# Zero point terms written ahead of a pair's products, and four token tiles transposed by DMA

## The chip, the cores and the metric

The kernel runs on one core of one Trainium2 chip. The metric is the device time of one execution in microseconds (us). The core has a matmul engine (PE, also TensorE, with its weight loads listed as PEld), a vector engine (DVE, VectorE), a scalar engine (ACT, ScalarE), a general engine (POOL, GpSimd), and SP (SyncE), whose queue here only issues DMAs. Each engine works through its own instructions strictly in order and waits on semaphores for the others. A DMA is issued from the queue of SP or of ACT and moves its data beside the engines.

## The reference

For each of two batches, x has 1024 tokens of 2048 elements, and ctx is 2048 by 2048. The first step is a quantised product, the second a linear layer with low-rank additions:

```
q1 = fake_quant(layernorm(x), x1_scale, x1_zp)     # clip(round(v / s + z), 0, 255), then (q - z) * s
q2 = fake_quant(ctx, x2_scale, x2_zp)
x  = x + q1 @ q2                                    # K = 2048, N = 2048
z  = layernorm(x)
x  = x + z @ kernel + bias + B_eff (A_eff z) + B_sh (A_sh z)
```

The kernel has both quantised operands as whole numbers from 0 to 255 less 128, which bf16 holds exactly, so the product of the codes is exact. The zero points come in as a sum: with d1 = 128 - z1 and d2 = 128 - z2, the product of the true values is s1 * s2 times (the product of the codes, plus d1 times the sum of each column of q2's codes, plus d2 times the sum of each row of q1's codes, plus 2048 * d1 * d2). This addition is called the zero point term here.

## The kernel before

**Tiling.** The 1024 tokens of a batch are 8 token tiles of 128 (m = 0 to 7), in four groups g of two tiles (MG = 2). The 2048 columns are four blocks n of 512. x and the running result live in four buffers y[g]. All of a batch's ctx codes for one column block are in two big buffers c2[n]; two column blocks are held at a time.

**Preparing x** is `prep_x(b, m)`. DVE takes the statistics of the layer norm (L283) and works out a scale and an offset. ACT quantises the tile to eight bits (L295, into q8, of which there are two that take turns), then recentres each half of 1024 elements to bf16 (L298, into qh, of which there is one) and sums it on the way. PE transposes each half in eight blocks of 128 by 128 into a psum tile pt (L303), and DVE copies that to c1T[g] (L304), the left operand of the product. The two sums give r_s, the row part of the zero point term (L306 to L308).

**Preparing ctx** is `quantise` (ACT L314, then DVE L317), eight calls for one column block, each on a 512 KB load that SP's queue issues ahead into ten buffers `lit`; `load_next` issues the next load when one is used up. `column_term` sums the columns on PE (pcp, L333), copies them with DVE (L343), adds the four partial sums on PE (pc, L345) and writes the column part of the zero point term to colt[n] with DVE (L348).

**The product** is `xattn_pair(b, n, g)`: one psum tile pa of two halves, one for each token tile j of the group. ACT writes the zero point term colt[n] + r_s[m] into a half (L359, at high priority), and 16 bf16 matmuls of 128x128 by 128x512 add to what stands there (L361, start=False). DVE adds the scaled pair to y (L370) and takes statistics of the result. Three psum tiles (acc1, delta, acc0) take turns for the pairs.

**The layer after it** is `ffn`: f32 matmuls of 128x128 by 128x512 (L611) in a seven by seven scheme of products of sums of blocks; o counts the outer products and s the inner ones. DVE spreads each result into y (L629), and finished blocks are sent to `out` by DMAs from ACT's queue (L631). While the layer of batch 0 ends (o = 6), `meanwhile` prepares batch 1: tiles m = 0 to 3 of x at s = 1 to 4, the ctx codes of its first column block at s = 0 to 3, its column term at s = 3, and the codes of the next block at s = 4 to 6. After it come the pairs of batch 1, with tiles 4 to 7 prepared between the pairs of column blocks 0 and 1, as in batch 0.

**What sets the order.** The Python code is written in one sequence, but a scheduler at build time decides the order in each engine's queue, by readiness and priority, with dependencies tracked by tile. The order is then fixed in the program; on the chip every queue keeps it.

Of the kernel before, what the change touches and what calls it, by code (L numbers as in the profile page):

```python
# [66 lines left out]
def tile_quant_xattn_then_lora_ffn(  # L67
# [17 lines left out]
    nc = tc.nc  # L85
    B, S, D = x.shape
    KT = D // P
    MT = S // P
# [8 lines left out]
    MG = GT // P  # L97
    H = D // 2
    KH = KT // 2
# [36 lines left out]
    def bf(t, n):  # L136

        return t.rearrange("p k n -> p (k n)").bitcast(BF16).rearrange("p (k n) -> p k n", n=n)

    def flat(t):  # L140
        return t.rearrange("p k n -> p (k n)")
# [87 lines left out]
    for tag in ("acc0", "acc1", "delta"):  # L229
# [11 lines left out]
        out=gate_b.rearrange("p b n -> p (b n)"),  # L241
        in_=gate.rearrange("b n -> (b n)").partition_broadcast(P),
# [11 lines left out]
    def norm_stats(stats, name):  # L254

        mv = small.tile([P, 2], F32, tag="mv", name=f"mv_{name}")
        nc.vector.bn_aggr(mv, stats.rearrange("p n s -> p (n s)"))
        ve = small.tile([P, 1], F32, tag="ve", name=f"ve_{name}")
        nc.vector.tensor_scalar_add(ve, mv[:, 1:2], EPS)
        sd = small.tile([P, 1], F32, tag="sd", name=f"sd_{name}")  # L260
        nc.scalar.activation(sd, ve, AF.Sqrt)
        r0 = small.tile([P, 1], F32, tag="r0", name=f"r0_{name}")
        nc.vector.reciprocal(r0, sd)

        t = small.tile([P, 1], F32, tag="nt", name=f"nt_{name}")
        nc.vector.scalar_tensor_tensor(t, ve, r0, r0, ALU.mult, ALU.mult)
        nc.vector.tensor_scalar(t, t, -0.5, 1.5, ALU.mult, ALU.add)
        rstd = small.tile([P, 1], F32, tag="rstd", name=f"rstd_{name}")
        nc.vector.tensor_mul(rstd, r0, t)
        return mv[:, 0:1], rstd  # L270
# [6 lines left out]
    def prep_x(b, m, c1T, wk):  # L277

        nm = f"{b}_{m}"
        g, tok = m // MG, ds((m % MG) * P, P)  # L280
        ym = y[g][:, m % MG, :]
        for n in range(NN):
            nc.vector.bn_stats(st1[:, m, n, :], ym[:, ds(n * NB, NB)])  # L283
        mean, rstd = norm_stats(st1[:, m], f"a{nm}")

        k = small.tile([P, 1], F32, tag="kx", name=f"kx_{nm}")
        nc.vector.tensor_mul(k, rstd, inv1)
        o = small.tile([P, 1], F32, tag="ox", name=f"ox_{nm}")
        nc.vector.tensor_mul(o, mean, k)
        nc.vector.tensor_sub(o, z1, o)  # L290

        wf = flat(wk)
        q8 = wf[:, ds((m % 2) * (D // 4), D // 4)].bitcast(U8)
        qh = wf[:, D // 2 : D].bitcast(BF16)
        nc.scalar.activation(q8, ym, AF.Identity, bias=o, scale=k)  # L295
        rsum = small.tile([P, 2], F32, tag="rsum", name=f"rsum_{nm}")
        for h in range(2):
            nc.scalar.activation(  # L298
                qh[:, ds(h * H, H)], q8[:, ds(h * H, H)], AF.Identity, bias=n_centre, accum_out=rsum[:, h : h + 1]
            )  # L300
            pt = ps_m.tile([P, KH, P], BF16, tag="pm", name=f"pt_{nm}_{h}")
            for kt in range(KH):
                nc.tensor.transpose(pt[:, kt, :], qh[:, ds(h * H + kt * P, P)], ident_h)  # L303
            nc.vector.tensor_copy(c1T[g][:, ds(h * KH, KH), tok], pt)  # L304

        r_c = small.tile([P, 1], F32, tag="r_c", name=f"r_c_{nm}")  # L306
        nc.vector.tensor_add(r_c, rsum[:, 0:1], rsum[:, 1:2])
        nc.vector.tensor_mul(r_s[:, m : m + 1], r_c, d2)  # L308
# [41 lines left out]
    def xattn_pair(b, n, g, c1T, c2):  # L350

        cols = ds(n * NB, NB)
        pairs.append((b, n, g))
        pa = ps_acc.tile([P, MG, NB], F32, tag=("acc0", "acc1", "delta")[len(pairs) % 3], name=f"pa_{b}_{n}_{g}")
        for j in range(MG):

            m = g * MG + j
            with tc.high_priority():
                nc.scalar.activation(pa[:, j, :], colt[n], AF.Identity, bias=r_s[:, m : m + 1])  # L359
            for k in range(KT):  # L360
                nc.tensor.matmul(  # L361
                    pa[:, j, :],
                    c1T[g][:, k, ds(j * P, P)],
                    c2[k // 8][:, k % 8, :],
                    start=False,
                    stop=(k == KT - 1),
                    skip_group_check=True,
                )
        yp = y[g][:, :, cols]
        summed = nc.vector.scalar_tensor_tensor(yp, pa, s12, yp, ALU.mult, ALU.add)  # L370
        for j in range(MG):
            nc.vector.bn_stats(st2[:, g * MG + j, n, :], y[g][:, j, cols])
        return summed
# [307 lines left out]
    c1T = [bf(t, GT) for t in c1T_bufs]  # L681
# [11 lines left out]
    for b in range(B):  # L693
# [6 lines left out]
        if b == 0:  # L700
            open_c2(0)
            prep_x(0, 0, c1T, wk)
            for r in range(NR):
                quantise(c2[0], r)
                if r == 3:
                    prep_x(0, 1, c1T, wk)
            for m in range(4, MT):
                load_x(0, m)
            open_c2(1)
            column_term(b, 0, c2[0])  # L710
        opened = xattn_pair(b, 0, 0, c1T, c2[0])
        if b == 0:
            for r in range(4):
                quantise(c2[1], r)
            for m in (2, 3):
                prep_x(b, m, c1T, wk)
        xattn_pair(b, 0, 1, c1T, c2[0])
        if b == 0:
            for r in range(4, NR):
                quantise(c2[1], r)  # L720
            column_term(b, 1, c2[1])
        for g in range(2):
            xattn_pair(b, 1, g, c1T, c2[1])
# [131 lines left out]
        if b + 1 < B:  # L855
            c1T_bufs, c1T, wk = state["c1b"], state["c1T"], state["wk"]
# [53 lines left out]
```

## Time and profile before

| | before |
|---|---|
| time, median of 3 runs | 1128.51 us (1127.28 to 1128.93) |
| profiled execution, its own time | 1128.61 us |
| span of the profiled execution | 1126.8 us |
| granted PE clock, mean | 0.999 |
| PE busy | 1072.4 us (95%) |
| DVE busy | 741.5 us (66%) |
| ACT busy | 261.1 us (23%) |
| POOL busy | 266.6 us (24%) |
| DMA, mean | 232 GB/s |

The profile is of one execution. A line such as `L303 PE MATMUL pt<-ident_h,big ...` names the line of the kernel, the engine, the operation and the tiles that it writes and reads; `x256` is how many there are. In a group the two numbers after the bar are the busy time of all and the mean of one in ns, and after the second bar stands the time in which the engine was idle just before them and what ended most of it. In a timeline the two first numbers are the start and the duration of a merged run of like instructions, in us from the span's start, and the brackets tell the idle time before it. Matmuls of a stream overlap, so the mean of one is longer than the distance from one to the next. "SPq" and "ACTq" are the issues of DMAs from the two queues. Batch 0's quantised product takes the first 200 us or so, its linear layer goes on to about 589 us, batch 1 follows.

### The profile page before, as it was taken

The numbers are of one execution on the slowest core, as the hardware profiler recorded it, in microseconds if no ns is written. First come the engines' busy times: TensorE is split into PE (matmuls) and PEld (weight loads), VectorE is DVE, ScalarE is ACT, GpSimd is POOL, SyncE is SP. The second block draws the span as 40 slices with busy tenths as digits, with TensorE's granted clock in tenths as the row PEclk, the third lists the DMA queues.
The fourth block names the chain that finished last, engine by engine and source line by source line (L and its number), as shares of the span: only waits on it lengthen the run. The fifth ranks groups of instructions, "written<-read, shape, count | busy, mean of one in ns | idle before, by whom it ended". The sixth has DMA issues, their size and how long they took to land.

```text
span 1126.8 us, 10619 instructions
## 1 busy us (share of the span) xinstructions
PE 1072.4 (95%) x3926; PEld 489.3 (43%) x3926; DVE 741.5 (66%) x969; ACT 261.1 (23%) x342; POOL 266.6 (24%) x106
## 2 busy tenths in 40 slices
PE   1689899999999999999999999999999999999998
PEld 0244334554444444444444433455444444444443
DVE  4685547576696768568777654766668586865861
ACT  5875513320001010001375761232000000000000
POOL 0000000234253422525000000022535343243600
PEclk9999999999999999999999999999999999999999
DMA  8991935885789757489857094588668875749611
GB/s 307 391 244 35 282 124 217 298 322 205 246 285 377 266 181 264 141 301 355 285 184 228 1 277 154 182 301 314 244 215 293 295 255 181 256 145 322 213 38 56
DMA packets 120772, 261.35 MB, mean 232 GB/s; under 512 B 11920, under 2 KB 16144, under 8 KB 119568
## 3 DMA queue, kind: packets, MB, share of 16 engines
q1 hardware_dynamic: 99264, 218.65, 56.6%
q10 hardware_dynamic: 21456, 42.02, 10.5%
q8 instruction: 31, 0.51, 0.2%
q14 instruction: 21, 0.17, 0.0%
HBM read 224.99 MB, written 37.75 MB: 233 GB/s over the span
## 4 chain that ended last, share of the span: by engine, by line
PE 80%; DMA 7%; DVE 6%; ACT 4%; issue 1%; SPq 1%; ACTq 0%; DVEq 0%
PE fu L611 33%; PE fv L611 17%; PE pa L361 13%; PE fw L611 9%; DMA lit<-in_ctx_dram 4%; PE pl L483 3%; PE ptz L432 2%; DVE big L560 1%; PE pg_a L383 1%; DVE st L283 1%; PE pg_b L383 1%; ACT big L298 1%; ACT big L295 1%; DMA bd<-q2b 1%; DMA big<-in_w_dram 1%
## 5 line engine op out<-in xcount | busy, mean ns | idle before, releaser
L611 PE MATMUL fu<-big,lit 128*128 128x512 f32 x896 | 396.3, 594 | 2.4 <-DVE y L629 2.4
L560 POOL TENSOR_TENSOR lit<-lit,lit 128x1024 f32<-128x1024 f32 x56 | 165.2, 2957 | 539.4 <-PE pa L361 209.1
L611 PEld LDWEIGHTS fu<-big,lit 128*128 128x128 f32 x896 | 167.8, 190 | 208.2 <-issue 206.7
L361 PE MATMUL pa<-big,big 128*128 128x512 bf16 x1024 | 238.0, 382 | 11.9 <-ACT pa L359 10.6
L611 PE MATMUL fv<-big,lit 128*128 128x512 f32 x448 | 198.1, 594 | 0.0
L551 POOL TENSOR_TENSOR lit<-lit,lit 128x1024 f32<-128x1024 f32 x40 | 100.9, 2524 | 283.4 <-DMA lit<-zs 255.5
L560 DVE TENSOR_TENSOR big<-big,big 128x2048 f32<-128x2048 f32 x56 | 159.4, 2850 | 5.9 <-PE ptz L432 5.3
L361 PEld LDWEIGHTS <-big 128*128 128x128 bf16 x1024 | 97.0, 98 | 146.5 <-issue 44.3
L629 DVE TENSOR_TENSOR y<-y,fu 128x1024 f32<-128x1024 f32 (+1 forms) x98 | 113.7, 1194 | 67.2 <-PE fu L611 66.8
L611 PEld LDWEIGHTS fv<-big,lit 128*128 128x128 f32 x448 | 84.3, 190 | 105.0 <-issue 105.0
L629 DVE TENSOR_TENSOR y<-y,fv 128x1024 f32<-128x1024 f32 x48 | 56.8, 1218 | 91.1 <-PE fv L611 91.1
L478 ACT COPY pl<-bias 128x1024 f32<-128x1024 f32 x32 | 32.6, 1017 | 344.9 <-DVE y L493 327.1
L314 ACT ACTIVATE q2b<-lit,sc,inv 128x1024 int16<-128x1024 f32 x64 | 76.6, 1230 | 146.4 <-DMA lit<-in_ctx_dram 124.7
L551 DVE TENSOR_TENSOR big<-big,big 128x2048 f32<-128x2048 f32 x40 | 101.7, 2544 | 13.2 <-DMA big<-in_w_dram 13.2
L611 PE MATMUL fw<-big,lit 128*128 128x512 f32 x224 | 100.6, 596 | 0.1
L370 DVE SCALAR_TENSOR_TENSOR y<-pa,k_s,y 128x1024 f32<-128x1024 f32 x32 | 41.0, 1282 | 69.7 <-PE pa L361 69.7
L359 ACT ACTIVATE pa<-bp,r_s 128x512 f32<-128x512 f32 x64 | 42.8, 684 | 105.6 <-PE pa L361 60.5
L629 DVE TENSOR_TENSOR y<-y,fw 128x1024 f32<-128x1024 f32 x24 | 28.4, 1217 | 52.5 <-PE fw L611 52.5
L611 PEld LDWEIGHTS fw<-big,lit 128*128 128x128 f32 x224 | 41.3, 190 | 48.7 <-issue 48.2
L303 PE MATMUL pt<-ident_h,big 128*128 128x128 bf16 x256 | 20.3, 231 | 29.6 <-ACT big L298 29.4
L283 DVE BATCH_NORM_STATS2 st<-y 128x6 f32<-128x512 f32 x64 | 42.1, 680 | 2.9 <-DMA y<-in_x_dram 2.9
L317 DVE TENSOR_SCALAR big<-q2b 128x1024 bf16<-128x1024 int16 x64 | 27.6, 440 | 23.7 <-ACT q2b L314 20.5
(79 smaller groups left out, 609.9 us busy)
## 6 DMA issues: line engine op xcount, KB each, us to landing
big<-in_w_dram SPq DMA_DIRECT2D x96, 1024.0 KB
lit<-zs SPq DMA_DIRECT2D x88, 512.0 KB
lit<-in_ctx_dram SPq DMA_DIRECT2D x64, 512.0 KB
out_dram<-y ACTq DMA_DIRECT2D x30, 512.0 KB
zs<-lit ACTq DMA_DIRECT2D x24, 512.0 KB
y<-in_x_dram SPq DMA_DIRECT2D x8, 1024.0 KB
lit<-in_lora_a_dram SPq DMA_DIRECT2D x32, 256.0 KB
lit<-in_lora_bt_dram SPq DMA_DIRECT2D x32, 256.0 KB
```

The costliest lines, as they stand in the source:

```text
L283: nc.vector.bn_stats(st1[:, m, n, :], ym[:, ds(n * NB, NB)])
L314: nc.scalar.activation(qi, t, AF.Relu, bias=z2, scale=inv2)
L317: nc.vector.tensor_scalar(c2[r // 4][:, ds(2 * (r % 4), 2), :], qi, QMAX, CENTRE, ALU.min, ALU.subtract)
L359: nc.scalar.activation(pa[:, j, :], colt[n], AF.Identity, bias=r_s[:, m : m + 1])
L361: nc.tensor.matmul(pa[:, j, :], c1T[g][:, k, ds(j * P, P)], c2[k // 8][:, k % 8, :], start=False, stop=(k == KT - 1), skip_group_check=True,)
L370: summed = nc.vector.scalar_tensor_tensor(yp, pa, s12, yp, ALU.mult, ALU.add)
L478: nc.scalar.copy(pl, self.bb.unsqueeze(1).to_broadcast([P, 2, NB]))
L483: nc.tensor.matmul(pl[:, i, ds(h * (NB // 2), NB // 2)], axT[rows, pr, ds(j * P, P)], self.bp[rows, ds(h * (NB // 2), NB // 2)], start=Fal ...
L551: line(eng.tensor_tensor(got[0], got[0], got[1], ALU.add if terms[1][2] > 0 else ALU.subtract))
L560: line(eng.tensor_tensor(out_t, at[p], at[q], op))
L611: nc.tensor.matmul(ps[:, m, :], at[:, k, ds(m * P, P)], bt[:, k, :], start=(opens and k == 0), stop=(ends and k == KQ - 1), skip_group_che ...
L629: line(nc.vector.tensor_tensor(yp, yp, chains[chain][:, js, :], ALU.add if sign > 0 else ALU.subtract))
```

## The change

In `xattn_pair` both token tiles' zero point terms are written before the first of the two products, where each product followed its own term. In `prep_x`, for the second batch and its tiles 0 to 3, each half of the centred tile is transposed by one DMA from ACT's queue, from qh to c1T (128 by 1024 elements of bf16, 256 KB), in place of eight transposes on PE, a psum tile and a copy on DVE. Eight DMAs take the place of 64 transposes and 8 copies. All other tiles are transposed on PE as before.

```diff
@@ prep_x @@
             nc.scalar.activation(
                 qh[:, ds(h * H, H)], q8[:, ds(h * H, H)], AF.Identity, bias=n_centre, accum_out=rsum[:, h : h + 1]
             )
+            if b > 0 and m < MT // 2:
+
+                nc.scalar.dma_start_transpose(out=c1T[g][:, ds(h * KH, KH), tok], in_=qh[:, ds(h * H, H)])
+                continue
             pt = ps_m.tile([P, KH, P], BF16, tag="pm", name=f"pt_{nm}_{h}")
             for kt in range(KH):
                 nc.tensor.transpose(pt[:, kt, :], qh[:, ds(h * H + kt * P, P)], ident_h)
@@ xattn_pair @@
             m = g * MG + j
             with tc.high_priority():
                 nc.scalar.activation(pa[:, j, :], colt[n], AF.Identity, bias=r_s[:, m : m + 1])
+        for j in range(MG):
             for k in range(KT):
                 nc.tensor.matmul(
                     pa[:, j, :],
```

## The prediction

> **What bounds the kernel now.** I read the page's busy times first, then the slices, the chain, the costliest groups, and after that the waits and the timeline of the two stretches that the change touches. The busy times and the chain:
>
> ```profile
> span 1126.8 us, 10619 instructions
> PE 1072.4 (95%) x3926; PEld 489.3 (43%) x3926; DVE 741.5 (66%) x969; ACT 261.1 (23%) x342; POOL 266.6 (24%) x106
> ...
> PE   1689899999999999999999999999999999999998
> ...
> PE 80%; DMA 7%; DVE 6%; ACT 4%; issue 1%; SPq 1%; ACTq 0%; DVEq 0%
> ```
>
> TensorE is the bound: 95% busy, and the digits below 9 stand only in the first 150 us. All else is worth what it does to PE's idle time or PE's work. The groups that the change touches:
>
> ```profile
> L361 PE MATMUL pa<-big,big 128*128 128x512 bf16 x1024 | 238.0, 382 | 11.9 <-ACT pa L359 10.6
> L359 ACT ACTIVATE pa<-bp,r_s 128x512 f32<-128x512 f32 x64 | 42.8, 684 | 105.6 <-PE pa L361 60.5
> L303 PE MATMUL pt<-ident_h,big 128*128 128x128 bf16 x256 | 20.3, 231 | 29.6 <-ACT big L298 29.4
> ```
>
> PE waits 10.6 us in all for zero point terms. The waits of PE between 0 and 210 us, then between 550 and 770 us (engine and line, for whom: us in total, times, longest), say where:
>
> ```profile
> PE pt L303 <- ACT big L298: 27.5, 2, 19.6
> PE pa L361 <- ACT pa L359: 9.8, 8, 2.2
> ```
> ```profile
> PE pt L303 <- ACT big L298: 2.0, 3, 0.8
> PE pa L361 <- ACT pa L359: 0.8, 1, 0.8
> ```
>
> So the terms cost 9.8 us in the first batch and 0.8 us in the second. The timeline of PE (start, us, what; in brackets idle before) shows the first pairs, and that transposes now slip between products at 0.066 us each (1.06 us for 16):
>
> ```profile
> 42.31 5.53 PE L361 MATMUL pa<-big,big 128*128 128x512 bf16 x16 [1.91 <-ACT pa L359]
> 48.62 3.61 PE L361 MATMUL pa<-big,big 128*128 128x512 bf16 x16 [0.78 <-ACT pa L359]
> 52.07 1.06 PE L303 MATMUL pt<-ident_h,big 128*128 128x128 bf16 x16
> ...
> 79.80 3.61 PE L361 MATMUL pa<-big,big 128*128 128x512 bf16 x16
> 83.25 0.78 PE L303 MATMUL pt<-ident_h,big 128*128 128x128 bf16 x11
> 83.87 1.67 PE L361 MATMUL pa<-big,big 128*128 128x512 bf16 x7
> 85.39 0.61 PE L303 MATMUL pt<-ident_h,big 128*128 128x128 bf16 x8
> 85.83 3.62 PE L361 MATMUL pa<-big,big 128*128 128x512 bf16 x16
> ```
>
> **Part one, both terms first.** No instruction is added: 64 terms of 0.684 us and 1024 matmuls stay. What goes is the wait of the second token tile's product, whose term could only be written once its psum half was reached in order. What comes is a new wait: the order of a psum tile's accesses is kept for the pair, so a pair's first matmul now waits for both terms, hence also for r_s of the second token tile. PE runs its queue in order, and behind that matmul stand the transposes of the next tiles, for which ACT's centring (L298) and with it ACT's queue wait.
>
> As built, the changed kernel's PE order is blocky: 32 products of a pair stand together, and the transposes stand together between pairs. In batch 0 it runs: 32 products, transposes of tiles 2 and 3, 16 column matmuls, 32 products, pc, 64 products, transposes of tiles 4, 5 and half of 6, 64 products, the rest of 6 and 7. The centred x (qh) is a single buffer, so L298 of a tile waits for the transposes of the tile before it. I walk it with the row durations (a product of 16: 3.46 to 3.6 us; L298: 1.1 per half; L295: 2.1; term: 0.68):
>
> - First pair: term j0 ends at 42.3, an L314 of 1.2 stands behind it, then term j1: start 44.0 for 42.3. The 0.78 of the second product goes. Net about +0.8 at the end of the pair (5.5 + 3.5 after 44.0 is 53.0 for 52.2).
> - Second pair and first pair of column block 1: term j1 stands on ACT behind L298 of tile 3 and two L314; pa_0_0_1 ends near 66.8 for 64.4. Then pc, the DVE's 0.8 (L348) and three terms in a row on ACT (j0, the next pair's j0, j1: 2.0 us) precede pa_0_1_0: 70.8 for 67.5, +3.3. The 0.84 of its second half goes: after 64 products (13.9) and the 16 transposes of tile 4, 85.7 for 83.4, +2.3.
> - Now nothing stands between the transposes of tile 4 and those of 5 and 6: PE waits for L298 of tile 5 (2.2), transposes, L298 of tile 6's first half (1.1). ACT then has L295 of tile 7 (2.1) ahead of the pair's second term (0.7): products start at about 91.4 to 91.8. Of these 6 us PE works 24 x 0.066 = 1.6; about 4.3 us are new idle time, where before 23 products covered it. Now +6.5.
> - Tile 7's last half again waits for transposes and is followed by r_s and term j1: about 0.8 more, +7.
> - Waits that go later: 0.78 at 115.6 and 2.16 at 128.8 us (there term j1 was queued behind an L314 that waited for ctx), and 0.29 at 89.7. If all go, batch 0 ends at about +4. If chains are 1 us shorter, +2; if the late waits stay, +7.
>
> The rest of batch 0 has PE as its bound, so this is carried to the end.
>
> In batch 1 tiles 4 to 7 stand in the same blocky order; there was only 0.78 + 0.62 + 0.51 us of waiting before, since products filled the gaps. The same two chains cost 4.5 to 5 and 0.8 us, and 0.8 goes: +5.
>
> **Part two, eight DMA transposes.** Removed: 64 PE transposes (64 x 0.066 = 4.2 us of PE's work), the 0.82 us that the first waited at 565.1, and 8 DVE copies (8 x 0.68 = 5.4 us; DVE was 19.7 of 28 us busy between 562 and 590, so off the path). TensorE's granted clock is 1.00 in both stretches: no gain or loss there. The last FFN products of batch 0 end some 2.5 us earlier (586.5 for 589.0), as 48 transposes preceded the end (3.2 + 0.8), less about 1 us that pc of column block 0 now waits for a DVE copy.
>
> Added on ACT's queue: 8 transposes of 256 KB, each behind its L298, each holding ACT's queue for a time d, and each needing a landing time before L298 may write qh again and before products may read c1T. No row shows one. The nearest rows differ: plain issues on ACT's queue take 0.33 to 0.41 us; the issue on SP's queue of 256 KB that lands in 128-byte pieces (acat) took 0.59 us and, for the second, 7.09 us. A transpose writes 256-byte rows, so it lies between; I take 1.5 us for d and 3 us to land (the DMA slices of that acat stage fall through 147, 106 and 51 GB/s; 256 KB at their mean of 101 take 2.6 us, and a little to start). Bounds: d from 0.35 to 7.1, landing from 1 to 7.
>
> What stands behind a transpose on ACT, as built: between T of tiles 0 to 3 stand L295 and L298 of the next tile, the terms of pa_1_0_0 and pa_1_0_1, and six of the eight L314 of column block 1 come after T of tile 3, where two of these six had run by 581.6 before. SP's loads of ctx and x share semaphores with these DMAs and wait behind them in part. With d = 1.5: the first pair starts at about 586.5, needs tiles 0 and 1, runs 7 us; the second pair's terms follow the last FFN addition (589.0), L298 of tile 3 (2.2), one T (1.5), r_s and a term (1.5): 595.4, so PE waits about 1.9. Late L314 push pc_1_1 from 599.7 to 605.7 us; but before the change PE there had its pairs of block 0 done only by then too, and its column block 1 pairs end by 622.7, tile 4's transposes by 623.8, for 623.6 before. So part two nets nothing: 4.2 + 0.8 us gained, about 5 lost to waits at the junction. With d = 0.35 and a quick landing it gains 3; each us more of d or landing costs about 5 to 8, as four rounds of L298, T, landing run one after the other.
>
> Sum: +4 (batch 0) + 0 (junction) + 5 (tiles 4 to 7 of batch 1) = +9. On the profiled execution, 1126.8 span and 1.8 around it, 1128.6: 1137.6; it stands 0.1 above the median 1128.5, so 1137.5.
>
> [...]
>
> **Rivals.**
> 1. Faster. The blocky order matters little, as ACT is 23% busy and runs ahead, and the 10.6 us of waits and 5 us at the junction go. For it: in the second window PE waited for L298 only 2.0 us. Against it: those waits were covered by products that now stand later. If the first pair's joint wait (1.7) and the second's (3) remain: -10.6 - 5 + 4.7 = -11, 1117.5.
> 2. Transposes are slow. If d is the 7.09 us of the second acat load, eight hold ACT's queue for 57 us; with four L295 and eight L298 (17 us) from 564 the last is through at about 638 for 596: +42, plus the +9, less the junction waits it swallows: about +45, 1173. It decides from d of about 2.5 us.
> 3. Cancel. The chains of tiles 4 to 7 are 2 us shorter than I walked in each batch and the transposes are quick (-3): 1128.5 + 9 - 4 - 4 = about 1129.5.
>
> **How the numbers follow.** My forecast (some transposes' cost, blocky chains) has 0.68, faster 0.12, slow transposes 0.12, cancel 0.08. From part one +2+4 with -3 to part one +7+6 with d near 2.5 (+8 at the junction, +8 on landing) the forecast spans 1131 to 1158. A fifth may be left out: the range leaves out the faster rival and the upper half of the slow one, and takes in cancel: 1127 to 1165. No change within 0.2% (2.3 us, about what a measurement of this kernel tells) gets 0.05, faster 0.13, slower 0.82.
>
> **What would show it.** In the profile after: PE idle before transposes (L298) near 86 and 625 us of 3 to 5 us, and no term waits at 115 and 128 us; PE waits for terms once a pair in the first three pairs; transposes on ACT's queue with d near 1.5 us; FFN of batch 0 ending 2 us earlier relative to its start, and that lost again by tile 4. If the waits for L298 stay at 2 us after 60 us, part one is wrong; if ACT's queue shows d of 0.4 or 7 us, part two's size is.

## The result, and the profile after

The changed kernel takes 1142.29 us (median of 4 runs, 1141.96 to 1144.43) against 1128.72 us: a ratio of 1.0126 with a 95% interval of 1.0112 to 1.0139, so 13.6 us slower. The profiled execution took 1142.39 us, its span is 1140.6 us. The change added lines, so the kernels number the same code differently: the products are L361 before and L366 after, the terms L359 and L363, the transposes L303 and L307, their copies L304 and L308; in the experiments these numbers shift by a few again. On the page of the kernel after, the lines that answer to those shown of before:

```profile
span 1140.6 us, 10496 instructions
PE 1067.4 (94%) x3862; PEld 488.5 (43%) x3862; DVE 733.8 (64%) x961; ACT 260.8 (23%) x342; POOL 263.2 (23%) x106
...
PE   1587999899999999999997889989999999999998
...
L366 PE MATMUL pa<-big,big 128*128 128x512 bf16 x1024 | 239.1, 389 | 15.1 <-ACT pa L363 15.1
...
L307 PE MATMUL pt<-ident_h,big 128*128 128x128 bf16 x192 | 15.5, 234 | 36.6 <-ACT big L298 27.5
```

PE's work fell by 5.0 us, its idle time rose from 54.4 to 73.2 us: 18.8 more, 13.8 net, which is the difference of the spans. The digits below 9 now stand in two places, the first quarter and the middle, where batch 1 begins (the last slice is 8 in both kernels). Waits of PE for zero point terms grew from 10.6 to 15.1 us; the change was to remove them. The list of waits of PE between 0 and 210 us shows a kind that was not there before, the second one here:

```profile
PE pa L366 <- ACT pa L363: 9.7, 5, 3.7
PE pt L307 <- DVE big L308: 5.6, 5, 1.2
```

The timeline of PE in batch 0 (start, duration, count, idle before):

```profile
71.08 15.66 PE L366 MATMUL pa<-big,big 128*128 128x512 bf16 x64 [3.75 <-ACT pa L363]
86.57 1.06 PE L307 MATMUL pt<-ident_h,big 128*128 128x128 bf16 x16
88.71 0.61 PE L307 MATMUL pt<-ident_h,big 128*128 128x128 bf16 x8 [1.08 <-DVE big L308]
90.49 1.20 PE L307 MATMUL pt<-ident_h,big 128*128 128x128 bf16 x16 [1.18 <-DVE big L308]
93.34 15.31 PE L366 MATMUL pa<-big,big 128*128 128x512 bf16 x64 [1.64 <-ACT pa L363]
108.48 1.06 PE L307 MATMUL pt<-ident_h,big 128*128 128x128 bf16 x16
...
617.64 15.98 PE L366 MATMUL pa<-big,big 128*128 128x512 bf16 x64 [3.13 <-ACT pa L363]
...
640.22 13.97 PE L366 MATMUL pa<-big,big 128*128 128x512 bf16 x64 [1.64 <-ACT pa L363]
```

Three things are to be read here. The transposes stand in a block between two runs of 64 products, with 3.9 us of waiting in the block. The second run starts at 93.34. And both runs are slow: 64 products in a row take 13.97 us at 640.22 us of the same trace, but 15.66 and 15.31 here, and 15.98 at 617.64 us after a wait of 3.13 us. The granted clock of the same four runs accounts for that (stretch, its length, PE busy, granted clock, DMA share, GB/s); 15.49 x 0.89, 15.14 x 0.91 and 15.82 x 0.87 all come to 13.8, the length of the run at 1.00:

```profile
71.08:86.57 15.49, 15.49 (x64) 0.89 0.70 189
93.34:108.48 15.14, 15.14 (x64) 0.91 0.00 1
617.64:633.46 15.82, 15.82 (x64) 0.87 0.34 88
640.22:654.03 13.81, 13.81 (x64) 1.00 0.00 1
```

DVE's timeline tells why the transposes wait: the psum tiles that they need are freed by DVE's copies, which stand behind the pair's addition and between its statistics.

```profile
86.78 1.28 DVE L375 SCALAR_TENSOR_TENSOR y<-pa,k_s,y 128x1024 f32<-128x1024 f32 x1 [4.30 <-PE pa L366]
87.97 0.68 DVE L308 COPY big<-pt 128x1024 bf16<-128x1024 bf16 x1
88.57 1.27 DVE L377 BATCH_NORM_STATS2 st<-y 128x6 f32<-128x512 f32 x2
89.77 1.27 DVE L308 COPY big<-pt 128x1024 bf16<-128x1024 bf16 x2
```

The first copy ends at 88.65 and the next transposes start at 88.71; the second ends at 90.4, and they start at 90.49. L298's two halves had been done at 88.4 and 89.5, so DVE came last both times, by 0.3 and 1.0 us; without it most of the first wait would have been L298's. Where the first linear layer's step s = 3 ends, the kernel after is 8.1 us late (570.49 for 562.37 us); at the end of that layer 4.7 us (593.71 for 589.02); at the end, 13.8.

### The profile page after: what moved, and what is told of

The parts are those of the page before. It is cut to its first block, busy times and chain, and to the rows that moved or that the text cites. A ratio compares the mean times of both kernels' runs of the same rounds, so it can differ in the third digit from the quotient of the medians.

```text
span 1140.6 us, 10496 instructions
## 1 busy us (share of the span) xinstructions
PE 1067.4 (94%) x3862; PEld 488.5 (43%) x3862; DVE 733.8 (64%) x961; ACT 260.8 (23%) x342; POOL 263.2 (23%) x106
## 3 DMA queue, kind: packets, MB, share of 16 engines
q10 hardware_dynamic: 29904, 44.11, 11.5%
## 5 line engine op out<-in xcount | busy, mean ns | idle before, releaser
L565 POOL TENSOR_TENSOR lit<-lit,lit 128x1024 f32<-128x1024 f32 x56 | 164.5, 2946 | 521.8 <-DMA bd<-q2b 217.6
L366 PE MATMUL pa<-big,big 128*128 128x512 bf16 x1024 | 239.1, 389 | 15.1 <-ACT pa L363 15.1
L556 POOL TENSOR_TENSOR lit<-lit,lit 128x1024 f32<-128x1024 f32 x40 | 98.2, 2458 | 318.1 <-DMA lit<-zs 296.8
L366 PEld LDWEIGHTS <-big 128*128 128x128 bf16 x1024 | 100.5, 100 | 151.2 <-issue 47.6
L565 DVE TENSOR_TENSOR big<-big,big 128x2048 f32<-128x2048 f32 x56 | 157.6, 2817 | 5.9 <-PE ptz L437 5.3
L556 DVE TENSOR_TENSOR big<-big,big 128x2048 f32<-128x2048 f32 x40 | 99.6, 2490 | 15.4 <-DMA big<-in_w_dram 15.4
L363 ACT ACTIVATE pa<-bp,r_s 128x512 f32<-128x512 f32 x64 | 41.9, 678 | 81.7 <-DVE y L375 37.4
L307 PE MATMUL pt<-ident_h,big 128*128 128x128 bf16 x192 | 15.5, 234 | 36.6 <-ACT big L298 27.5
```

What stands on the lines that cost most here:

```text
L366: nc.tensor.matmul(pa[:, j, :], c1T[g][:, k, ds(j * P, P)], c2[k // 8][:, k % 8, :], start=False, stop=(k == KT - 1), skip_group_check=True,)
L556: line(eng.tensor_tensor(got[0], got[0], got[1], ALU.add if terms[1][2] > 0 else ALU.subtract))
L565: line(eng.tensor_tensor(out_t, at[p], at[q], op))
```

## The experiments

Times are medians; ratios are to the kernel before, run on the same chip.

**Each half alone.** e1 takes the second hunk of the change only, e2 the first only.

> Both terms ahead of both products, and no DMA transposes. Theory A (the order of the terms carries nearly all of the loss: it makes PE's queue blocky, so PE waits for DVE, ACT and, after the waits, runs at a lower granted clock): batch 0 unchanged from the kernel after, at +8 us where the first linear layer ends its s = 3 step; in all 1137 to 1141 us. Theory B (the DMA transposes and what they push back at the junction are a good half of the loss): 1133 to 1136 us.

> DMA transposes for the first four tiles of batch 1, and each term just ahead of its product as before. Theory A: the 4.2 us of PE transposes and the 0.8 us of waiting are gained, and late quantising of ctx and late terms at the junction give about as much back: 1127 to 1131 us, with issues of the transposes at 1.25 us each. Theory B: 1133 to 1137 us.

e1: 1139.04 us, ratio 1.0103 (1.0088 to 1.0118), +11.1 us. e2: 1132.12 us, ratio 1.0039 (1.0025 to 1.0053), +4.2 us. Together 15.3 for the 13.6 of both: nearly additive. The terms carry most of it, as theory A had it, but the DMA transposes are no even trade, as theory A and the prediction both had it. In e2's timeline the first linear layer of batch 0 ends 3.4 us earlier than before (585.58 us), and then PE waits:

```profile
595.87 0.39 PE L336 MATMUL pcp<-big,ones_h 128*32 128x512 bf16 x2 [1.14 <-DVE big L320]
...
606.33 1.10 PE L348 MATMUL pc<-q2b,mean_w 128*128 128x512 f32 x2 [1.66 <-DVE q2b L346]
609.34 12.43 PE L364 MATMUL pa<-big,big 128*128 128x512 bf16 x48 [1.91 <-ACT pa L362]
```

With two more of 0.28 and 0.46 these are 5.5 us, at work of ACT and DVE that now comes later: six of the eight L314 of column block 1 follow the last transpose. 48 products then take 12.43 us, where 47 x 0.216 + 0.38 = 10.5 is their pace (0.216 us from start to start in undisturbed runs, 0.38 for the last): 1.9 us more.

**Two buffers for qh.** The diff against the kernel after, for tiles 4 to 7 (q8 moves to one of the load buffers):

```diff
+        if m >= MT // 2:
+            q8 = flat(q8x[0])[:, ds((m % 2) * (D // 4), D // 4)].bitcast(U8)
+            qh = wf[:, ds((m % 2) * (D // 2), D // 2)].bitcast(BF16)
```

> The kernel after, with two buffers for the centred tile (qh) in tiles 4 to 7 of both batches, so that L298 of a tile no longer waits for the transposes of the tile before it. If PE's idle time between the transposes of tiles 4 to 7 comes from L298 and its single buffer, as the prediction had it, 3 to 4 us per batch go: 1134 to 1137 us. If it comes from DVE (a pair's addition, 1.28 us, and statistics, 1.29 us, stand ahead of the copies that free the transposes' psum tiles), PE still waits 1.1 to 1.2 us before each half for DVE and the time stays within 2 us of 1142.

1135.98 us, ratio 1.0076 (1.0057 to 1.0095): 6.3 us better than after. By the number that is the answer for L298's buffer, but the trace makes it unclear: the scheduler, seeing tile 5 ready sooner, put 6 products between its two halves, and where transposes still stand next to each other PE still waits 1.08 us for DVE (3.2 and 2.2 us in all in the two batches, 5.6 and 3.3 in the kernel after). So the edit changed the order too, and the two causes are not separated by it. e9 goes at the order itself.

**DMA transposes in another place.** Terms as before; `if m >= MT // 2:` in place of `if b > 0 and m < MT // 2:`.

> Terms as before; DMA transposes not for the first four tiles of batch 1 but for tiles 4 to 7 of both batches, where the DMA engines are idle (share 0.00 to 0.01 from 86 to 102 us). If what hurts a DMA transpose is other DMA traffic and ACT's work at the junction, this place gains: 128 PE transposes at 0.066 us are 8.4 us, and the time falls to 1120 to 1125 us. If what hurts is the chain (L298, two issues of 1.25 us, landing of 3 to 5 us, then L298 of the next tile), PE waits some 5 us per batch for c1T and the time is 1127 to 1133 us.

1128.79 us, ratio 1.0009 (0.9998 to 1.0020): no change that shows. 8.4 us of PE's transposes are gone, and so are some 2.1 us of work that the edit was not aimed at (the gated steps below, 27.4 us for 29.5); the waits that came take both: in batch 0

```profile
103.77 10.06 PE L364 MATMUL pa<-big,big 128*128 128x512 bf16 x38 [3.94 <-DMA big<-big]
```

and behind it ACT, in whose queue the issue of tile 6's two halves and the next L298 stand (start, duration, what):

```profile
96.06 1.33 ACTq L302 DMA_TRANSPOSE big<-big  x1
96.10 1.29 ACT L362 ACTIVATE pa<-bp,r_s 128x512 f32<-128x512 f32 x2
97.43 4.06 ACTq L302 DMA_TRANSPOSE big<-big  x1
103.74 1.15 ACT L298 ACTIVATE big<-big,n_centre 128x1024 bf16<-128x1024 uint8 x1 [6.36 <-DMA big<-big]
```

From the issue of the first half to the landing of the second it is 7.7 us. So the chain hurts away from the junction too. That other DMA traffic has no part in it is not shown: between 95 and 104 us loads of ctx and of the low-rank matrices moved another 1.57 MB. Nor is the junction cleared: there 8 DMAs cost 4.2 us (e2), here 16 cost nothing that shows.

The same trace has a run that is slow for no reason in its order, which up to there is that of before. The row of this run, then that of before:

```profile
67.43 13.93 PE L364 MATMUL pa<-big,big 128*128 128x512 bf16 x56 [2.15 <-ACT pa L362]
67.50 4.69 PE L361 MATMUL pa<-big,big 128*128 128x512 bf16 x21 [2.15 <-ACT pa L359]
```

Here 56 products take 1.7 us more than 55 x 0.216 + 0.38 = 12.3; in before, and in e2 and e7, the same wait costs nothing (20 x 0.216 + 0.38 = 4.7).

**Priority for the preparation of tiles 4 to 7**, on the kernel after (e5) and on e1 (e6):

```diff
-                with tc.issue_after(opened.ins):
+                with tc.issue_after(opened.ins), tc.high_priority():
                     prep_x(b, m, c1T, wk)
```

> The kernel after, with the preparation of tiles 4 to 7 at high priority in the scheduler, so that their transposes stand between products again (batch 1) or ahead of the pairs that need them (batch 0). If the loss of the terms' order is the place of these transposes, nearly all of the waits between 85 and 115 us and between 633 and 660 us go, and with them the slow products behind: 8 to 10 us in batch 1; in batch 0 a new wait of up to 5 us for x of tile 4, which is ready at 73 us only, takes part of 8 us back: 1127 to 1134 us. If the loss is the joint wait for both terms itself, it stays at 1139 to 1142 us.

> Terms ahead, no DMA transposes, tiles 4 to 7 prepared at high priority. Place of the transposes: 1124 to 1131 us for 1139 us of the terms alone. Joint wait: 1136 to 1139 us.

1144.95 us, ratio 1.0145 (1.0123 to 1.0166), and 1141.37 us, ratio 1.0106 (1.0084 to 1.0128). Both missed: the waits went where they were to go, and larger ones came. In e5, from the first product of column block 1 in batch 0 to the end of the pairs of tiles 4 to 7, PE is busy 37.83 of 38.00 us, where it was 44.76 of 51.10. But DVE now takes the statistics of tiles 4 to 7, from 54.3 to 67.8 us, ahead of tile 2's copies, and tile 3's transposes wait for the psum tiles that these free:

```profile
68.58 1.86 PE L307 MATMUL pt<-ident_h,big 128*128 128x128 bf16 x16 [14.67 <-DVE big L308]
```

So the test of the place was spoiled by the edit's own side effect; e9 repeats it with less.

**The gated step.** In the kernel after, a step's four small f32 matmuls (pg_a, pg_b: 32 columns each) mostly stand together, in the kernel before one of them stands apart from the other three in 12 of 16 steps. The timeline of before:

```profile
134.32 1.05 PE L383 MATMUL pg_a<-lit,gmat 128*32 128x512 f32 x2
135.30 3.63 PE L361 MATMUL pa<-big,big 128*128 128x512 bf16 x16
138.85 1.06 PE L383 MATMUL pg_a<-lit,gmat 128*32 128x512 f32 x6
139.84 2.33 PE L361 MATMUL pa<-big,big 128*128 128x512 bf16 x10
```

Each run takes 0.98 to 0.99 us till the next begins, whether one matmul (two records) or three stand in it. The edit in `gated`, against the kernel before:

```diff
-        for h in range(2):
-            buf, t = next_loaded()
-            for c in range(2):
+        got = [next_loaded() for _ in range(2)]
+        for h in (1, 0):
+            for c in (1, 0):
                 row = (2 * h + c) * GP
...
-                    t[:, c, :],
+                    got[h][1][:, c, :],
...
-            lit.give(buf)
-            load_next()
+        for buf, _ in got:
+            lit.give(buf)
+            load_next()
```

> The kernel before, with the four small f32 matmuls of a gated step (pg_a, pg_b) standing together on PE, as they do in most steps of the kernel after; nothing else is changed. In the trace of before one such matmul alone and three together take 0.98 us each, and all four together 1.00 us. If that is PE's time, 12 split steps give 12 x 0.98 = 11.8 us: 1115 to 1118 us. If the rows only show it so, the time stays at 1127 to 1129 us.

1119.69 us, ratio 0.9918 (0.9904 to 0.9932): 9.3 us faster than the kernel before, a good part of the 11.8, though above the 1115 to 1118 expected. The busy time of both groups fell from 29.5 to 17.0 us. In the profiled execution, which took 1124.26 us and was the slowest of its six, part was given back: the wait of 2.16 us at 128.83 us has become one of 2.94 us, and the 26 products behind it take 7.46 us where their pace makes 25 x 0.216 + 0.38 = 5.8. In the kernel after the same groups take 21.3 us, so the change carries a gain of up to 8.2 us of PE's time that nobody meant.

**Transposes from SP's queue.** As e2, with `nc.sync.dma_start_transpose`.

> DMA transposes alone, issued from SP's queue in place of ACT's, terms as before. If what the DMA transposes cost at the junction is ACT's queue held for 1.25 to 3.1 us by each issue, with six quantising steps of ctx pushed behind: 1125 to 1129 us, for 1132 us. If it is the time to land and the single qh buffer: 1131 to 1134 us.

1134.77 us, ratio 1.0054 (1.0037 to 1.0071), not better than e2. ACT's queue is free, but L298 of tile 2's second half now waits for the landing, and SP's loads of x stand behind the transposes (three of them hold SP's queue for 10.49 us). So it does not help to take the issues off ACT's queue: the time to land remains, and the loads behind the transposes are held in place of ACT. What each of the two costs was not separated.

```profile
581.37 1.15 ACT L298 ACTIVATE big<-big,n_centre 128x1024 bf16<-128x1024 uint8 x1 [5.55 <-DMA big<-big]
```

**The place of the transposes, alone.** The kernel after, with high priority only from L298 to the copy:

```diff
+        with tc.high_priority() if m >= MT // 2 else nullcontext():
             for h in range(2):
                 nc.scalar.activation(
...
```

> The kernel after, with high priority only from the centring (L298) of tiles 4 to 7 to the copy of their transposes, not for their statistics and quantising: the order up to the first pair of column block 1 is that of the kernel after, and from there each half's transposes stand between products. If the place of the transposes is what costs in tiles 4 to 7, the waits of 3.9 and 2.4 us in batch 0 and 3.9 and 2.9 us in batch 1 go, and the slow products behind them (2.6 us in batch 0), less 1 to 2 us of a new wait for L298 of tile 4: 1128 to 1133 us. If the joint wait for two terms costs there, it stays at 1139 to 1142 us.

1126.93 us, ratio 0.9991 (0.9977 to 1.0006), below both expectations: 15.4 us below the kernel after, more than the whole loss. Up to 71 us its order is that of the kernel after, the joint wait of 3.75 us included; then the transposes slip between products:

```profile
70.45 5.73 PE L367 MATMUL pa<-big,big 128*128 128x512 bf16 x18 [3.75 <-ACT pa L364]
76.20 0.62 PE L308 MATMUL pt<-ident_h,big 128*128 128x128 bf16 x8
76.66 0.59 PE L367 MATMUL pa<-big,big 128*128 128x512 bf16 x2
...
93.78 18.08 PE L367 MATMUL pa<-big,big 128*128 128x512 bf16 x83
```

From the joint wait to 112 us PE waits 0.46 us for L298 and for nothing else, and 83 products run at 0.216 us each. The size fits the trace of the kernel after: the waits between the transposes and ahead of the products behind them are 3.90 and 2.44 us in batch 0, 3.90 and 2.83 us in batch 1, and the products behind the waits of batch 0 lost 1.3 and 1.2 us, 15.6 in all. So in the kernel after the place of the transposes of tiles 4 to 7 costs more than the whole net loss. The joint waits for two terms do not explain it: they stand in e9 as they were, and PE's waits for terms still come to 11.0 us there.

**Two tiles only** (`m < MG` in place of `m < MT // 2` in e2), and the same with e7's edit:

> DMA transposes alone, and only of the first two tiles of batch 1 (4 DMAs); tiles 2 and 3 on PE, terms as before. If a DMA transpose costs by its rate (about 4 us each, one after the other, with L298 of the next tile and the second pair behind it), the first two tiles have the time, as their products start 20 us later: 32 transposes of 0.066 us and the 0.8 us wait are gained, 1124 to 1127 us. If each transposing DMA hurts by what it does to ACT's queue and the other DMAs, half of the loss of the four tiles stays: 1129 to 1131 us.

> The two changes of e7 and e10 in one kernel: the gated step's four matmuls together, and DMA transposes of the first two tiles of batch 1. If both hold and add: 1115 to 1119 us. If e10 gains nothing: 1119 to 1122 us.

e10: 1129.6 us, ratio 1.0009 (0.9996 to 1.0022), inside the second expectation (half of the loss stays), but not told apart from the kernel before; half the transposes cost nothing that shows and gain nothing. e11: 1118.02 us, ratio 0.9905 (0.9887 to 0.9923), the fastest here, but its interval and that of e7 overlap, so only e7's edit is shown to gain.

**The terms with the transposes placed**, gated steps together, no DMA transposes.

> The kernel before with the gated step's four matmuls together (e7), both terms ahead of both products, and tiles 4 to 7 transposed between products as in e9; no DMA transposes. It tells what the terms' order is worth where its side effect on the transposes is taken away. If the waits that it removes (0.78 us several times, 2.16 us at 128.8 us of before) outweigh the joint wait of the first pairs (3.65 and 3.75 us): 1114 to 1118 us. If the joint waits and the slow products behind them weigh more: 1121 to 1126 us, above the 1119.7 us of e7.

1134.77 us, ratio 1.0064 (1.0047 to 1.0081), above both expectations, and so no answer to the question asked. Up to 121 us it agrees with e9 within 0.15 us. Then a gated step waits for its own loads, 5.42 us at 129.47 and 3.33 us in batch 1, the 64 products behind each take 14.65 and 15.54 us for 13.99, and 5.4 us go to L298 in batch 1. The row of e9 and that of e12:

```profile
124.45 3.91 PE L389 MATMUL pg_a<-lit,gmat 128*32 128x512 f32 x8 [0.51 <-DMA lit<-in_lora_a_dram]
129.47 1.94 PE L385 MATMUL pg_a<-lit,gmat 128*32 128x512 f32 x8 [5.42 <-DMA lit<-in_lora_a_dram]
```

In e9 the step begins when the first of its loads is there and its four matmuls then run one after the other, in e12 it needs both before it begins; the products go on at 128.29 and 131.34 us. Two edits that gain alone did not add here. Against e1 this kernel gains 4.3 us, no more than its gated steps do (18.0 us for 22.3), so in a kernel without DMA transposes the place of the transposes is not shown to gain anything in the end. Why L298 of batch 1 comes late was not tried.

## Why the prediction was right, and where it was off

It forecast slower by 9 us, by blocky transposes in both batches and a junction that nets nothing. It was slower by 13.6, inside the range, and by that mechanism as to the blocks: e9 takes them away and with them 15.4 us. That the sum came within 4.6 us is partly luck: it left out 6.2 us of slow products and 2.1 us of waits at the junction on one side, and a gain of up to 8.2 us on the other. Point by point:

- **The first pairs** went as worked out: pa_0_0_0 from 43.2 to 52.6 us (44.0 to 53.0 forecast), pa_0_1_0 at 71.08 (70.8). The terms' waits are not removed but joined: 3.65, 0.51 and 3.75 us, one per pair.
- **Tile 4's transposes** were to end at 85.7 and ended at 87.5; the next pair was to start at 91.6 and started at 93.34. The size of the wait between is right (3.9 for 4.3 us), its cause only in part: 1.64 us are the terms behind L295, as walked, but the other 2.26 us end with DVE's copies, not with L298. The 1.8 us come from what stands in no term of the sum: the 64 products after the wait of 3.75 us ran slow, 15.66 us for 13.97. The granted clock over this run is 0.89. The sum had "TensorE's granted clock is 1.00 in both stretches: no gain or loss there" from the trace of before, where no wait behind the first products is longer than 2.2 us. That trace should have warned: its clock record says 1.00 there too, yet its first row of products, shown in the prediction, takes 5.53 us for 3.61 behind a wait of 1.91; in the kernel after the record has 0.73 at that place. This is the term that failed: 1.7, 1.3 and 1.2 us in batch 0 (the last on the 32 products at 114.05 us, 8.29 for 7.07) and 2.0 in batch 1, together 6.2 us. Behind the longer waits the losses measured are 2.5 us behind the first joint wait of 3.65, 1.7 behind that of 3.75, 2.0 behind 3.13 and, in e7, 1.7 behind 2.94. Shorter waits do not agree among themselves: 1.7 us went behind one of 2.15 us in e4 and 1.9 behind one of 1.91 us in e2, nothing behind 2.15 and 2.16 us in before. The run at 93.34 had three waits of 1.1 to 1.6 us before it and lost 1.3, while the one at 640.22 had the same three and lost nothing: the length of one wait alone does not decide, and what does is not shown here.
- **Tile 7's chain** was put at 0.8 us and L298; it took 2.4 us in batch 0 (1.08, 1.18 and 0.18) and 2.8 in batch 1, and DVE. Here too the cause of the waits was misplaced: the forecast walked ACT's queue and left out DVE's, on which an addition and two statistics stand ahead of the copies as soon as a pair ends just before the transposes. The sum had the copies "off the path".
- **Batch 0** was to end at +4; it was +8.1 at s = 3.
- **The later waits** of 0.78 and 2.16 us went, as forecast; gated steps wait for loads in their place, 1.34 us at 135.56 and 1.14 at 679.67.
- **The junction.** The issue d was put at 1.5 us and is 1.25 (up to 3.1 for the second of a pair); the landing, put at 3, is later: from the start of the second half's issue to the L298 that waits for the transposes pass 5.6 to 5.9 us in the kernel after and in e2, 6.3 and 6.9 in e4. pa_1_1_0 was forecast at 608.8 and comes at 617.64, 609.5 less batch 0's 8.1. The step that fell short is "so part two nets nothing": alone it costs 4.2 us (e2), of which 2.1 are the waits less the gain and 1.9 the slow products behind them. Two halves, 16 blocks of 128x128, took 7.7 us in e4, 0.48 us a block, with other loads in flight.
- **Not seen at all**: the gated steps standing together, up to 8.2 us of gain. Without it the kernel would have been up to 22 us slower. With it the ledger of the kernel after nearly closes: 15.4 (place of the transposes) + 4.2 (DMA) - 8.2 (gated) leave 2.2 us of the 13.6. The joint waits may be that rest, as e9's column sum of block 2 comes 2.3 us later than before (120.47 for 118.21 us); this is argued, not shown. The ledger does not carry over: by it e12, with 11.5 us less in its gated steps and neither block nor DMA, would take about 1119 us, and it took 1134.8.
- **The rivals.** "Faster" needed ACT to run ahead; the waits it counted as gone turned into others. "Slow transposes" with d = 7 us is out, d is 1.25. "Cancel" is out; its sum also takes 4 us for the quick transposes where its text has 3, so it should have read 1130.5.

What stays open: whether L298's buffer or DVE's copies would set the block's length if the other were gone (e3 changed the order too), what the terms' order is worth by itself (e12 met other waits), and when PE's clock falls behind a wait.

## What to carry to other kernels

A wait that is taken out of an in-order queue had a use if the scheduler filled it: here the gaps between the two products of a pair were where the next tiles' transposes stood, and with the gaps gone the transposes stood in a row, behind each other's psum tiles and another engine's queue. So compare the order on each engine first, look for runs of small work that used to be mixed with large work, and walk every queue that frees a buffer for them, not only the one that feeds them. If the order is what fails, give priority to just those instructions (e9) and not to all that precedes them (e5), and measure the whole: in e12 the same priority was eaten up by waits further on.

## What the runs showed of the hardware

- Small f32 matmuls (128*32 by 128x512) into different strips of 32 rows of one psum tile took the time of one where they stood together in the kernel before: 0.98 us for one, 0.99 for three, 1.00 for four. Grouping 12 split steps gave 9.3 us (e7). Where the step had to wait for its loads they did not: four that stood together took 3.91 us at 124.45 us in e9.
- A DMA transpose of 128 by 1024 bf16 elements took 1.25 us of ACT's queue (median in the kernel after; up to 3.1 there and 4.1 in e4 for the second of a pair) and 5.6 to 6.9 us from the second half's issue to use (after, e2, e4), with other loads in flight. On PE the same eight blocks took 0.46 us until the next product begins (76.20 to 76.66 us in e9).
- After a wait of 2.94 to 3.75 us, PE lost 1.6 to 2.5 us over the next work (1.6 in e12 after 3.33, 2.5 after the 3.65 us ahead of the first pair of the kernel after, 9.59 us for 7.07); after one of 2.15 us it lost 1.7 us in e4 and nothing in before, e2 and e7, with the same order up to there; three waits of 1.1 to 1.6 us cost 1.3 us once and nothing the other time.
- The granted clock on record did not always show this: in the kernel before it is 1.00 over the 16 products that took 5.53 us for 3.61.
